# Two blocks of cross attention and experts: where scratch rows are cleared, and how the first context is loaded and normalized

## The chip, the core and the metric

The kernel runs on one core of a Trainium2 chip. The number that counts is the device time of one execution in microseconds (us); lower is better. The core has a matrix engine (TensorE, "PE" in the profile, its weight loads "PEld"), a vector engine (VectorE, "DVE"), a scalar engine (ScalarE, "ACT") and GpSimd ("POOL"). SyncE ("SP") computes nothing here: its instruction queue issues most of the DMA transfers. ACT and POOL issue some as well, from their own queues. All transfers run on the same 16 DMA engines.

## The reference, cut to what matters

```python
x = x + xattn0(ctx, layernorm(x))        # 8 heads of 128; keys from ctx and from x
x = x + experts0(layernorm(x))           # 8 experts, the best 2 of each token, capacity 1024
x = x + xattn1(ctx, layernorm(x))        # 8 heads of 32
x = x + experts1(layernorm(x))           # 8 experts, the best 2 of each token, no capacity
# inside xattn0, for each of 4 batches:
xn, ln = norm(ctx) * gm + bm, norm(latents) * gl + bl
q = ln @ Wq + bq
k, v = split(concat([xn, ln]) @ Wkv + bkv)
out = softmax(q k^T * 128**-0.5) v @ Wo + bo
```

There are 4 batches of 512 rows of x (width 256) and 4 contexts of 1601 rows. Everything is float32. In the first expert layer a slot that no token fills counts as a row of zeros, and in the second each expert's rows have a variable number. So the kernel keeps three scratch arrays in DRAM, which are cleared before tokens are scattered into them.

## The kernel before, in words

The kernel has four stages, one after the other, all in one program.

- **Opening** (lines 541 to 816). Loads of weights, context 0 and x; layer norm of x twice (once for the block, once inside the attention; the result is called lat) and of the 13 tiles of 128 context rows; transposes of both into `kvin`; queries and keys of head 0.
- **First attention** (loop from line 825). A step is one tile of 128 queries of one head of one batch: 4 x 8 x 4 = 128 steps. A step computes `scores` on PE (L735), a row maximum on DVE (L743), the exponential on ACT (L749), then `exchange`: 16 transfers that swap blocks of 32 rows between partitions (L756; 12 issued by SP, 4 by ACT). One step later `turn` transposes the swapped blocks on DVE (L764). `weigh` multiplies a pair of turned tiles with the values (L772, PE). The scores have one PSUM buffer, so scores of a step wait for the exponential of the step before. PE's other work is put between: queries and keys of the next head (L670, L685), values of a pair of heads (L718) and the output projection (L783). The list `later[n]` holds what is added to step n.
- **First experts** (loop at line 1023). For each expert: load `sx`, its 512 slots, from `slot_x` (L1026), transpose, hidden layer (L970), results of the expert before (L983), and two weight loads of 1 MB for the next expert (L909, L910). Results go to `slot_y`.
- **Second attention and second experts** follow. The second experts take rows from `rows_a` and `rows_b`, which are scattered during the second attention.

Three scratch arrays are cleared at the end of the opening. `clear_rows` (L370 to L380) sends 4 transfers of 530 KB for `rows_a` and 37 for `rows_b` from SP, out of a zero tile of 4 x 265 numbers per partition. `clear_slots` (L179) sends 8 transfers of 512 KB for `slot_x` from POOL. The arrays are 19.8, 2.2 and 4.2 MB (`rows_b`, `rows_a`, `slot_x`).

The code does not fix every engine's order. A list scheduler arranges each engine's instructions ahead of the run, by dependencies and by durations that it assumes. Two helpers bind it: `in_order(*engines)` keeps what is traced inside it in program order on those engines, and `keep_in_program_order` puts one instruction behind the one traced before it on its engine. Neither adds a wait for completion. An engine's queue then runs strictly in that order.

The opening of before is free for the scheduler. It uses `ln_moments`, `ln_scale` and `ln_apply` (L111 to L149): statistics of all 13 context tiles, then one scale for all of them, then the normalization, all on DVE except one square root on ACT. The bias of the output is also worked out there: eight times a copy of a bias column over 128 columns (`values_bias`, L801) and a matmul pair with `wo` (L802), summed in one PSUM tile, added to `bo`, and `bo` added to x of batch 0 on POOL (L601).

`keys` (L681 to L697) takes four blocks of 512 contiguous columns of `kvin` and one of 128, and ACT writes each back permuted, since the key order in `kT` is by the position k of a column's 32-group within its block of 128.

Of the kernel before, what the change touches and what calls it, by code (L numbers as in the profile page):

```python
# [8 lines left out]
F32 = mybir.dt.float32  # L9
I32 = mybir.dt.int32  # L10
AF = mybir.ActivationFunctionType
ALU = mybir.AluOpType
# [50 lines left out]
def rows_of(i, n, tail):  # L63
    return tail if i == n - 1 else P
# [3 lines left out]
def xattn_ffn_twice(ctx: ExitStack, tc: tile.TileContext, a: dict, out: bass.AP):  # L68
# [107 lines left out]
    rows_a = dram.tile([E * G, PAY], F32, name="rows_a")  # L176
    rows_b = dram.tile([ROWS + G, PAY], F32, name="rows_b")

    def clear_slots(zeros):  # L179
        for i in range(SLOTS // (4 * P)):  # L180
            nc.gpsimd.dma_start(
                slot_x[i * 4 * P : (i + 1) * 4 * P, :].rearrange("(p r) d -> p r d", p=P), zeros
            )


    iota_i = const.tile([P, NT, E], I32, name="iota_i")
    nc.gpsimd.iota(iota_i, pattern=[[0, NT], [1, E]], base=0, channel_multiplier=0)
    iota = const.tile([P, NT, E], F32, name="iota")
    nc.vector.tensor_copy(iota, iota_i)
# [146 lines left out]
                )  # L336


    lane_i = const.tile([P, 1], I32, name="lane_i")
    nc.gpsimd.iota(lane_i, pattern=[[0, 1]], base=0, channel_multiplier=1)  # L340
    lane = const.tile([P, 1], F32, name="lane")
    nc.vector.tensor_copy(lane, lane_i)
    number_i = const.tile([P, NG], I32, name="number_i")
    nc.gpsimd.iota(number_i, pattern=[[1, NG]], base=0, channel_multiplier=0)
    number = const.tile([P, NG], F32, name="number")
    nc.vector.tensor_copy(number, number_i)
    full = const.tile([P, T // G], F32, name="full")
    nc.vector.tensor_scalar(full, number[:, : T // G], float(G), None, ALU.mult)
    notafter = const.tile([P, E, E], F32, name="notafter")
# [19 lines left out]

    def clear_rows(empty):  # L370

        nc.gpsimd.memset(empty, 0.0)
        nc.gpsimd.memset(empty[:, :, D : D + 1], NOWHERE)
        for rows in (rows_a, rows_b):
            n = rows.shape[0]
            for i in range(0, n, 4 * P):
                some = rows[i : min(i + 4 * P, n), :]
                nc.sync.dma_start(
                    some.rearrange("(p r) d -> p r d", p=P), empty[:, : some.shape[0] // P, :]
                )  # L380

    def route2(b, two, psum, tag, first=0, n=NT):

# [148 lines left out]
    with ExitStack() as st:  # L532
# [9 lines left out]
        gbl = w.tile([P, 2, DC], F32, name="gbl")  # L542
        bqk = w.tile([P, 3, H0], F32, name="bqk")
        bo = w.tile([P, D], F32, name="bo")
        for dst, names in (
            (gbm, ("gamma_media", "beta_media")),
            (gbl, ("gamma_lat", "beta_lat")),
            (bqk, ("bq", "bk", "bv")),
        ):
            for k, name in enumerate(names):  # L550
                nc.sync.dma_start(dst[:, k, :], a[name])
        nc.sync.dma_start(bo, a["bo"].partition_broadcast(P))

        kvin = one.tile([P, DC, NB, 4, 32], F32, name="kvin")
        nc.vector.memset(kvin[:, :, NB - 2 :, 3, :], 0.0)
# [12 lines left out]
            nc.sync.dma_start(t[:TAIL, NM - 1, :], a["ctx"][b, full:, :])  # L568
            return t

        ctx_b = load_ctx(0)

        wq = w.tile([P, DC, INNER], F32, name="wq")
        wkv = w.tile([P, DC, 2 * INNER], F32, name="wkv")
        wo = w.tile([P, H0, D], F32, name="wo")
        nc.sync.dma_start(wq, a["wq"].rearrange("(c p) f -> p c f", p=P))
        nc.sync.dma_start(wkv, a["wkv"].rearrange("(c p) f -> p c f", p=P))
        nc.sync.dma_start(wo, a["wo"].rearrange("(h p) d -> p h d", p=P))
        for b in range(1, B):
            load_x(b)  # L580
        nc.sync.dma_start(wr, a["w_router"].rearrange("(c p) e -> p c e", p=P))
        nc.sync.dma_start(bias, a["bias"].partition_broadcast(P))

        def keys_input(b, ctx_b):

# [11 lines left out]

            def latents_again():
                layernorm(two, state["lat"], state["lat"], NT)
                for i in range(NT):  # L600
                    nc.gpsimd.tensor_tensor(x[b][:, i, :], x[b][:, i, :], bo, ALU.add)  # L601

            def apply(n0):
                for i in range(n0, min(n0 + 4, NM)):
# [38 lines left out]
            def ctx_group(n0):  # L643
                group(ctx_b, n0, min(4, NM - n0), S + n0 * P, gbm, TAIL, NM)


            early = [
                lambda: moments(range(4)),
# [12 lines left out]
        def queries_keys(h):  # L661

            qT = two.tile([P, S], F32, tag="qT", name="qT")
            kT = two.tile([P, LP], F32, tag="kT", name="kT")
            hs = slice(h * DH0, (h + 1) * DH0)

            def queries():
                ps = ps_t.tile([P, 512], F32, tag="t", name="ps_q")
                for c in range(DC):
                    nc.tensor.matmul(  # L670
                        ps,
                        lhsT=wq[:, c, hs],
                        rhs=kvin[:, c, : S // 32, 0, :],
                        start=c == 0,
                        stop=c == DC - 1,
                    )
                nc.vector.tensor_scalar(
                    qT, ps, bqk[:, 0, h : h + 1], DH0**-0.5, ALU.add, ALU.mult
                )

            def keys(j0):  # L681
                n = min(512, LP - j0)
                ps = ps_t.tile([P, 512], F32, tag="t", name="ps_k")
                for c in range(DC):
                    nc.tensor.matmul(  # L685
                        ps[:, :n],
                        lhsT=wkv[:, c, hs],
                        rhs=flat_kvin[c][:, j0 : j0 + n],
                        start=c == 0,
                        stop=c == DC - 1,  # L690
                    )
                nc.scalar.activation(  # L692
                    kT.rearrange("p (k b i) -> p b k i", k=4, i=32)[:, j0 // P : (j0 + n) // P],
                    ps[:, :n].rearrange("p (b k i) -> p b k i", k=4, i=32),
                    AF.Identity,
                    bias=bqk[:, 1, h : h + 1],
                )  # L697

            return qT, kT, [queries] + [lambda j0=j0: keys(j0) for j0 in range(0, LP, 512)]


        parts = (range(0, NB // 2 + 1), range(NB // 2 + 1, NB))
# [77 lines left out]
        def project(oT, inv, h, b, half):  # L780
# [9 lines left out]
            for k in range(2):  # L790
# [3 lines left out]
                    xs, ps[:, k, :], inv[:, t : t + 1], xs, ALU.mult, ALU.add  # L794
                )


        values_bias = w.tile([P, P], F32, name="values_bias")
        ps = ps_t.tile([P, D], F32, tag="t", name="ps_bo")
        for h in range(H0):  # L800
            nc.vector.tensor_copy(values_bias, bqk[:, 2, h : h + 1].to_broadcast([P, P]))  # L801
            nc.tensor.matmul(  # L802
                ps, lhsT=values_bias, rhs=wo[:, h, :], start=h == 0, stop=h == H0 - 1
            )
        nc.vector.tensor_tensor(bo, bo, ps, ALU.add)

        early, late = keys_input(0, ctx_b)
        for s in early + late:
            s()
        *qk, fill = queries_keys(0)  # L810
        for s in fill:
            s()
        empty = one.tile([P, 4, PAY], F32, tag="lat", name="empty")
        clear_rows(empty)
        clear_slots(empty[:, :, :D])
        load_second()

# [1 line left out]
        later = [[] for _ in range(n_steps + 4)]  # L821
        tiles = {}
        v_of = [None, None]
        early = late = ()
        for n in range(n_steps + 4):
            b, h, t = n // (H0 * NT), n // NT % H0, n % NT
# [166 lines left out]
    with ExitStack() as st:  # L993
# [20 lines left out]
        def results(e, hT, w2):  # L1014
# [4 lines left out]
                slot_y[e * CAP : (e + 1) * CAP, :].rearrange("(t p) d -> p t d", p=P), y  # L1019
            )  # L1020

        last = None
        for e in range(E):
            w1, w2 = w_next
# [9 lines left out]
            last = (e, hT, w2)  # L1034
            if e + 1 < E:
                w_next = expert_weights(wexp, "w1", "w2", e + 1)
        results(*last)

        got0, steps = collect(0)
        for f in steps:  # L1040
# [721 lines left out]
```

## Time and profile before

| | us |
|---|---|
| median of 3 runs | 2993.43 (2989.96 to 2995.0) |
| the profiled execution's own time | 2993.88 |
| its span | 2992.2 |
| PE busy in the span | 2778.0 (93%) |
| DVE busy | 1456.4 (49%) |
| ACT busy | 933.3 (31%) |
| first scores of the first attention start | 53.06 |
| first attention ends, first experts begin (about) | 1635 |
| first hidden layer of the first experts starts | 1706.9 |
| last result of the first experts lands (about) | 1939 |

The profiled execution is within 0.5 us of the median. Its own time is 1.7 us above its span, for what lies around it. PE busy says how long PE had a matmul in flight, not that it ran at its peak. A row of a group gives line, engine, tile written and tiles read, number of instructions, busy time, and the idle time of the engine just before them with what ended it. A queue's row (SPq, ACTq) gives the time in which that queue was issuing transfers, not the time of the transfer itself.

### The profile page before, as it was taken

The numbers are of one execution on the slowest core, as the hardware profiler recorded it, in microseconds if no ns is written. First come the engines' busy times: TensorE is split into PE (matmuls) and PEld (weight loads), VectorE is DVE, ScalarE is ACT, GpSimd is POOL, SyncE is SP. The second block draws the span as 40 slices with busy tenths as digits, with TensorE's granted clock in tenths as the row PEclk, the third lists the DMA queues.
The fourth block names the chain that finished last, engine by engine and source line by source line (L and its number), as shares of the span: only waits on it lengthen the run. The fifth ranks groups of instructions, "written<-read, shape, count | busy, mean of one in ns | idle before, by whom it ended". The sixth has DMA issues, their size and how long they took to land.

```text
span 2992.2 us, 35534 instructions
## 1 busy us (share of the span) xinstructions
PE 2778.0 (93%) x13426; PEld 1839.3 (61%) x13426; DVE 1456.4 (49%) x2324; ACT 933.3 (31%) x1312; POOL 400.0 (13%) x308
## 2 busy tenths in 40 slices
PE   5699999999999999999997999879989898898998
PEld 2466676667766667666665566634444444466887
DVE  4256447544475444554454200178777768741110
ACT  2133234323343233333331221124434344341221
POOL 1000000100001000000000100022314223333442
PEclk9899999999999999999998899979999999898999
DMA  8743334433344333333334333110101110055552
GB/s 297 236 124 95 98 92 103 117 92 89 95 113 109 90 94 91 99 93 97 95 94 120 117 106 115 47 46 17 28 24 41 29 37 23 11 181 169 185 173 72
DMA packets 165103, 295.95 MB, mean 99 GB/s; under 512 B 43287, under 2 KB 81752, under 8 KB 161848
## 3 DMA queue, kind: packets, MB, share of 16 engines
q1 hardware_dynamic: 124024, 204.45, 24.4%
q0 software_dynamic: 16320, 53.42, 5.9%
q10 hardware_dynamic: 24576, 35.68, 4.6%
q8 instruction: 109, 1.79, 0.3%
q14 instruction: 74, 0.61, 0.1%
HBM read 97.86 MB, written 49.76 MB: 49 GB/s over the span
## 4 chain that ended last, share of the span: by engine, by line
PE 82%; DVE 7%; issue 3%; DMA 3%; ACT 3%; SPq 2%; POOL 1%; POOLq 0%; DVEq 0%; ACTq 0%
PE ps_o L772 15%; PE ps_s L735 15%; PE ps_v L718 7%; PE ps_k L685 7%; PE ps_w L1188 6%; PE ps_y L1470 4%; PE ps_h L1451 4%; PE ps_h L970 4%; PE ps_y L983 4%; DVE tops L1149 2%; PE ps_o L1219 2%; DVE sum L1210 2%; PE ps_p L783 2%; PE ps_v L945 2%; PE ps_q L670 2%
## 5 line engine op out<-in xcount | busy, mean ns | idle before, releaser
L743 DVE TENSOR_REDUCE top<-ps_s 128x1 f32<-128x2113 f32 x128 | 301.8, 2358 | 574.8 <-PE ps_s L735 574.8
L772 PE MATMUL ps_o<-pT,v 128*128 128x256 f32 x2176 | 521.5, 382 | 7.7 <-DVE pT L764 7.7
L735 PE MATMUL ps_s<-kT,qT 128*128 128x512 f32 (+1 forms) x1280 | 488.9, 527 | 26.3 <-ACT attn L749 26.0
L772 PEld LDWEIGHTS ps_o<-pT,v 128*128 128x128 f32 x2176 | 411.4, 191 | 124.8 <-issue 70.3
L735 PEld LDWEIGHTS ps_s<-kT,qT 128*128 128x128 f32 x1280 | 241.8, 191 | 275.7 <-issue 239.9
L749 ACT ACTIVATE attn<-ps_s,top 128x2113 f32<-128x2113 f32 x128 | 259.0, 2024 | 486.5 <-DVE top L743 448.8
L764 DVE STREAM_TRANSPOSE pT<-swapped 128x2176 f32<-128x2176 f32 x128 | 312.4, 2441 | 70.8 <-DMA swapped<-attn 60.3
L1149 DVE TENSOR_REDUCE tops<-ps_s 128x2 f32<-128x1024 f32 (+1 forms) x224 | 237.4, 1104 | 135.2 <-PE ps_s L1138 135.0
L685 PE MATMUL ps_k<-kvin,wkv 128*128 128x512 f32 (+1 forms) x640 | 262.0, 534 | 5.0 <-ACT kT L692 5.0
L1188 PE MATMUL ps_w<-asked,keyed 64*128 64x256 f32 (+1 forms) x1664 | 244.2, 415 | 20.5 <-DVE tops L1149 9.5
L718 PE MATMUL ps_v<-wkv,kvin 128*128 128x256 f32 x1088 | 253.5, 381 | 0.0
L1201 ACT ACTIVATE pT<-ps_w 128x1024 f32<-128x1024 f32 (+1 forms) x176 | 179.5, 1024 | 192.5 <-PE ps_w L1188 190.4
L1188 PEld LDWEIGHTS ps_w<-asked,keyed 64*128 64x128 f32 (+1 forms) x1664 | 147.0, 189 | 143.2 <-ACT pT L1201 60.7
L718 PEld LDWEIGHTS ps_v<-wkv,kvin 128*128 128x128 f32 x1088 | 204.9, 190 | 32.7 <-issue 3.3
L1210 DVE TENSOR_TENSOR sum<-sum,pT 128x1024 f32<-128x1024 f32 (+1 forms) x128 | 181.0, 1414 | 10.7 <-ACT pT L1201 3.9
L692 ACT ACTIVATE kT<-ps_k,bqk 128x512 f32<-128x512 f32 (+1 forms) x160 | 97.3, 621 | 268.7 <-DMA swapped<-attn 129.8
L1210 POOL TENSOR_TENSOR sum<-sum,pT 128x1024 f32<-128x1024 f32 x48 | 124.1, 2585 | 345.7 <-ACT pT L1201 345.5
L685 PEld LDWEIGHTS ps_k<-kvin,wkv 128*128 128x128 f32 x640 | 116.5, 192 | 80.9 <-issue 67.1
L1451 PE MATMUL ps_h<-xT,w_e 128*128 128x256 f32 x640 | 143.9, 383 | 10.2 <-issue 10.2
L1138 PE MATMUL ps_s<-kT,qT 32*128 32x512 f32 (+1 forms) x1024 | 140.5, 577 | 12.5 <-ACT kT L936 6.8
L725 ACT COPY v<-ps_v 128x512 f32<-128x512 f32 x144 | 80.0, 561 | 224.9 <-PE ps_v L718 156.2
L1470 PE MATMUL ps_y<-w_e,hT 128*128 128x256 f32 x640 | 144.4, 385 | 0.0
(261 smaller groups left out, 2615.1 us busy)
## 6 DMA issues: line engine op xcount, KB each, us to landing
swapped<-attn SPq DMA_DIRECT2D x1536, 68.0 KB
swapped<-attn ACTq DMA_DIRECT2D x512, 68.0 KB
rows_b<-empty SPq DMA_DIRECT2D x36, 530.0 KB
w<-in_w_dram SPq DMA_DIRECT2D x16, 1024.0 KB
w_e<-in_wall_dram SPq DMA_DIRECT2D x7, 2052.0 KB
cT<-in_ctxT_dram SPq DMA_DIRECT2D x4, 1601.0 KB
keyed<-kT SPq DMA_DIRECT2D x32, 200.1 KB
ctx_b<-in_ctx_dram SPq DMA_DIRECT2D x4, 1536.0 KB
```

The costliest lines, as they stand in the source:

```text
L685: nc.tensor.matmul(ps[:, :n], lhsT=wkv[:, c, hs], rhs=flat_kvin[c][:, j0 : j0 + n], start=c == 0, stop=c == DC - 1,)
L718: nc.tensor.matmul(ps[:, k, :], lhsT=flat_kvin[c][:, j * P : (j + 1) * P], rhs=wkv[:, c, cols], start=c == 0, stop=c == DC - 1,)
L735: nc.tensor.matmul(flat[:, j0 : j0 + n], lhsT=qT[:, t * P : (t + 1) * P], rhs=kT[:, j0 : j0 + n], start=True, stop=True,)
L743: nc.vector.tensor_reduce(top, flat[:, :L], AX.X, ALU.max, negate=True)
L749: nc.scalar.activation(attn[:, :L], flat[:, :L], AF.Exp, bias=top, accum_out=total)
L764: nc.vector.transpose(pT[:, :, k * P : (k + 1) * P].rearrange("p c (a i) -> p a c i", a=4), swapped.rearrange("p a (c i) -> p a c i", i=32),)
L772: nc.tensor.matmul(ps, lhsT=v[:, j - parts[part][0], (h % 2) * DH0 : (h % 2 + 1) * DH0], rhs=pT[:, j, :], start=j == 0, stop=j == NB - 1,)
L1149: nc.vector.tensor_reduce(tops[u][:, t : t + at // n, 2 * pair : 2 * pair + 2, j0 // 512], of, AX.X, ALU.max,)
L1188: nc.tensor.matmul(ps[:r, s, pair * QH : (pair + 1) * QH], lhsT=keyed[o][64 * s : 64 * s + 64, pair, j * P : j * P + r], rhs=asked[u % 3][ ...
L1210: (nc.gpsimd if k else nc.vector).tensor_tensor(to, to, pT[:r], ALU.add)
L1451: nc.tensor.matmul(ps[:, f, :], lhsT=w(at, P), rhs=xT[:, c, :], start=c == 0, stop=c == DC - 1,)
L1470: nc.tensor.matmul(ps, lhsT=hT[:, f, r * P : (r + 1) * P], rhs=w(WB1 + f * D, D), start=f == 0, stop=f == FC - 1,)
```

## The change

The clearing of the three scratch arrays is put elsewhere, and the opening is written anew.

- `clear_slots` is now called eight times, in steps 4, 6, ... 18 of the first attention, and issued by SP instead of POOL, each call pinned behind SP's instruction traced before it. The zeros are one tile of 256 numbers per partition, repeated four times by the transfer.
- `clear_rows` is now a generator. The loop over the first experts takes six of its 41 transfers after the weight loads of each next expert. They stay on SP, pinned in the same way; the zeros are one row of 265 numbers per partition, repeated four times.
- The loads of the opening are traced in a given order on SP: x, the first four context tiles, the small vectors, the columns of head 0 of `wq` and `wkv`, the other context tiles, then the remaining weights, x of the other batches and the router.
- Layer norm of context 0 is done in groups of four tiles (`first`): statistics and scale on DVE, the normalization itself on ACT (scale and bias of one ACTIVATE).
- PE, DVE, ACT and POOL run the opening in program order. Keys are cut by k, so that the first block of keys needs the latents alone.
- The bias of the output, with its eight copies and matmul pairs and the POOL addition for batch 0, moves to step 13 of the first attention.
- Three small integer tiles get a pool of their own that is closed early.

```diff
-    def clear_slots(zeros):
-        for i in range(SLOTS // (4 * P)):
-            nc.gpsimd.dma_start(
-                slot_x[i * 4 * P : (i + 1) * 4 * P, :].rearrange("(p r) d -> p r d", p=P), zeros
+    def clear_slots(zeros, i):
+        tc.keep_in_program_order(
+            nc.sync.dma_start(
+                slot_x[i * 4 * P : (i + 1) * 4 * P, :].rearrange("(p r) d -> p r d", p=P),
+                zeros.unsqueeze(1).to_broadcast([P, 4, D]),
             )
...
     def clear_rows(empty):
-        nc.gpsimd.memset(empty, 0.0)
-        nc.gpsimd.memset(empty[:, :, D : D + 1], NOWHERE)
...
-                nc.sync.dma_start(
-                    some.rearrange("(p r) d -> p r d", p=P), empty[:, : some.shape[0] // P, :]
-                )
+                tc.keep_in_program_order(
+                    nc.sync.dma_start(
+                        some.rearrange("(p r) d -> p r d", p=P),
+                        empty.unsqueeze(1).to_broadcast([P, some.shape[0] // P, PAY]),
+                    )
+                )
+                yield
...
+        loading.enter_context(in_order(nc.sync))
+        for n0 in range(0, NM - 1, 4):
+            nc.sync.dma_start(ctx_b[:, n0 : n0 + 4, :], of_ctx[:, n0 : n0 + 4, :])
+            if n0 == 0:
+                load_vectors(gbl, "gamma_lat", "beta_lat")
+                load_vectors(bqk, "bq", "bk", "bv")
+                nc.sync.dma_start(wq[:, :, :DH0], of_wq[:, :, :DH0])
+                nc.sync.dma_start(wkv[:, :, :DH0], of_wkv[:, :, :DH0])
+                load_vectors(gbm, "gamma_media", "beta_media")
+        nc.sync.dma_start(ctx_b[:TAIL, NM - 1, :], a["ctx"][0, (NM - 1) * P :, :])
+        nc.sync.dma_start(wkv[:, :, INNER:], of_wkv[:, :, INNER:])
+        nc.sync.dma_start(wq[:, :, DH0:], of_wq[:, :, DH0:])
+        nc.sync.dma_start(wkv[:, :, DH0:INNER], of_wkv[:, :, DH0:INNER])
...
+            def first(n0):
+                n = min(4, NM - n0)
+                mv = two.tile([P, 4, 2], F32, tag="mv4", name="mv_g")
...
+                for i in range(n):
...
+                    nc.vector.bn_stats(st[:r], ctx_b[:r, n0 + i, :])
+                    nc.vector.bn_aggr(mv[:r, i, :], st[:r])
+                mv, rs = ln_scale(two, mv, 4)
+                away = two.tile([P, 4], F32, tag="nt4", name="away")
+                nc.vector.scalar_tensor_tensor(away, mv[:, :, 0], -1.0, rs, ALU.mult, ALU.mult)
+                for i in range(n):
...
+                    nc.scalar.activation(
+                        of, of, AF.Identity, scale=rs[:r, i : i + 1], bias=away[:r, i : i + 1]
+                    )
...
-            def keys(j0):
-                n = min(512, LP - j0)
+            def keys(k):
+                n = 512 if k < 4 else P
...
-                        rhs=flat_kvin[c][:, j0 : j0 + n],
+                        rhs=kvin[:, c, : NB - 1, k, :] if k < 4 else kvin[:, c, NB - 1, :, :],
...
-        early, late = keys_input(0, ctx_b)
-        for s in early + late:
+        opening.enter_context(in_order(*computing))
+        latent, context = keys_input(0, ctx_b)
+        *qk, fill = queries_keys(0)
+        stats, turns = context[::2], context[1::2]
+        for s in (
+            latent[:2] + stats[:1] + latent[2:] + fill[:2] + stats[1:2] + turns[:1] + stats[2:3]
+            + turns[1:2] + fill[2:3] + stats[3:] + turns[2:3] + fill[3:4] + turns[3:] + fill[4:]
+        ):
             s()
...
-        clear_rows(empty)
-        clear_slots(empty[:, :, :D])
...
+        for i in range(SLOTS // (4 * P)):
+            later[4 + 2 * i].append(lambda i=i: clear_slots(empty, i))
+        later[13].append(output_bias)
...
+        clear = clear_rows(empty)
         last = None
         for e in range(E):
...
             if e + 1 < E:
                 w_next = expert_weights(wexp, "w1", "w2", e + 1)
+                for _ in range(6):
+                    next(clear, None)
         results(*last)
```

In the order of the opening, `latent` is the layer norm, the second layer norm and the transposes of the latents, `stats` the four groups `first`, `turns` the transposes of the four groups, and `fill` the queries and the five blocks of keys of head 0.

## The prediction, made before the changed kernel was run

> **What bounds the kernel now.** I read the chain of waits first, cut to the first stretch, because the page's share of "DMA 3%" is a mean over four unlike stages.
>
> ```profile
> by line: DMA rows_b<-empty 25.7%; SPq L378 25.6%; PE ps_s L735 14.8%; PE ps_o L772 8.1%; DMA swapped<-attn 6.9%; ACT attn L749 4.7%; PE ps_k L685 4.3%; DVE top L743 3.9%; SPq L756 3.4%; issue 2.5%; PE ps_p L783 0.8%; ACTq L749 0.1%
> ...
> 44.59 18.01 DMA rows_b<-empty
> ...
> 62.62 12.86 DMA rows_b<-empty
> ...
> 100.49 1.25 SPq L378
> ...
> 101.84 6.37 DMA swapped<-attn
> ```
>
> This is the chain from 40 to 160 us (start, length, what). Half of it is the clearing of `rows_b`: SP is issuing those transfers until 101.8, and only then the first exchange. The timeline shows who pays:
>
> ```profile
> 53.06 3.87 PE L735 MATMUL ps_s<-kT,qT 128*128 128x512 f32 x10 [0.33 <-ACT kT L692]
> ...
> 65.48 6.27 ACTq L756 DMA_DIRECT2D swapped<-attn  x4
> ...
> 71.81 1.26 ACT L692 ACTIVATE kT<-ps_k,bqk 128x512 f32<-128x512 f32 x2 [9.76 <-DMA swapped<-attn]
> ...
> 80.57 14.97 PE L718 MATMUL ps_v<-wkv,kvin 128*128 128x256 f32 x68
> ...
> 101.84 33.56 SPq L756 DMA_DIRECT2D swapped<-attn  x42
> 115.11 2.44 DVE L764 STREAM_TRANSPOSE pT<-swapped 128x2176 f32<-128x2176 f32 x1 [31.99 <-DMA swapped<-attn]
> ...
> 117.33 5.83 PE L735 MATMUL ps_s<-kT,qT 128*128 128x512 f32 x10 [18.35 <-ACT attn L749]
> ```
>
> ACT is held in its own queue while DMA is full, keys wait for ACT; `turn` waits 32 us; PE stands still 18.35 us. Last, the windows (length, then busy time of PE, PEld, DVE, ACT, POOL, then PE clock, DMA share, GB/s):
>
> ```profile
> 53.06:141.80 88.74, 59.66 (x185) 36.40 (x185) 20.78 (x15) 20.65 (x28) 0.00 (x0) 0.85 0.81 280
> ...
> 200.00:400.00 200.00, 200.00 (x743) 137.12 (x742) 111.23 (x153) 67.71 (x91) 2.97 (x4) 1.00 0.41 103
> ...
> 1740.00:1760.00 20.00, 19.99 (x77) 13.40 (x76) 1.96 (x4) 3.29 (x6) 0.00 (x0) 1.00 0.37 114
> ```
>
> After 141.8 PE is never idle in the attention, so time lost before it comes off the end in full, and work added to PE is added in full. The first experts (last line) are PE-bound with DMA 37% busy.
>
> **What the Trainium skill says.** "DMA: Bandwidth & Descriptors", section Queues, rings and completion order: on each DMA engine the descriptors of one queue are consumed in ring order. The trace agrees: exchanges came behind the clears on SP. Its section Issuing engines are not separate DMA queues says all issuers share 16 engines; agreed: ACT's four transfers took 6.27 us to issue at 65.48 and 2.71 at 141.77. "ScalarE: Activation LUTs", section Table sets, says identity is in every table set, so the new ACTIVATE between square roots loads no table; the trace has Identity (L630) between a root and the load at 53.28, with no load of its own. "TensorE: Matmul & The Clock Gate", What's actually happening, says PE is at half clock after about 3.4 us idle; here the ten score matmuls took 5.83 us after the 18 us stall against 3.87 before.
>
> **Step 1, stall in the first steps.** From 53.06 to 141.80 PE computed, counted at the pace of the undisturbed stretch (from 153.90 a score group starts the next after 3.60; four key matmuls 1.72, eight value matmuls 1.73, six `ps_o` 1.29): five score groups 18.0, queries and keys (28 large matmuls of 0.43, four small of 0.11) 12.4, values (68 of 0.216) 14.7, `ps_o` (34 of 0.216) 7.3. Sum 52.4. Lost: 88.7 - 52.4 = 36.3 us.
> What is late next? The pipeline's own filling. A score cycle is 3.87 + 2.36 (maximum) + 2.1 (exponential) = 8.4 us. Counting from the first scores: exponential 0 ends at 8.4, keys of head 1 fill PE to about 9; scores 1 to 12.8; more keys to 16.8; exponential 1 ends at 17.4 (0.6 lost); scores 2 to 21; values fill 14.7, to 36. An exchange takes 9.7 us in the undisturbed part (exponential ends 141.75, `turn` at 151.47), so tile 1 is turned at about 30, before PE wants it. At least 0.6 us is lost. If the scheduler keeps the order of before (values and next queries ahead of scores 3, then scores 4 close behind), the gaps of 4.60 and 1.09 before 127.76 and 141.80 stay. I take 4, bounds 0.6 and 9. Gain: 32.3 (27.3 to 35.7).
>
> **Step 2, the opening.** In before DVE waits for context until 13.69, while x was in by about 4.3 (the windows show 376 GB/s in 3 to 4 us, then a lull of 21). After, DVE starts on x at 4.3. Rows: statistics 0.41 and aggregate 0.17 with the next overlapped, about 0.52 a tile; the chain of scale, 0.2 + root 0.24 + five small operations of 0.17, 1.27; application 0.34 a tile. One layer norm of x: 2.1 + 1.27 + 1.37 = 4.75; two end at 13.8. First context group on DVE 2.1 + 1.27 + 0.16 = 3.5, to 17.4; ACT applies four tiles at 0.36 (a COPY of 128x256 at 141.64) to 18.9, then the latents' half to 19.7 (0.78, L630). Queries 1.72 us on a warm PE; it had 8 transposes only, so half clock, 3.0, to 22.7; DVE writes them (0.75) by 23.5. Next group: DVE to 27.1, ACT to 28.5, evacuations (1.0 on each) to 29.5. Third: DVE to 31.6, ACT 33.1, evacuation 34.1; keys 1 to 35.9 and out by 36.7. The last tile's root stands behind that on ACT: applied by 38.3, evacuation of group 2 by 39.3; keys 2 to 41.1, last evacuation 42.6; keys 3 and 4 to 44.9, written by 45.5. First scores at 45.5 against 53.06: gain 7.5. Bounds: 42 (warm PE, overlap everywhere) and 50 (0.1 us more at each of some 40 hand-overs). The loads don't decide: 7.9 MB at some 380 GB/s are in by 25, values' weights needed beyond 65.
>
> **Step 3, the bias in step 13.** In before its matmuls lay in PE's idle opening. Now 16 matmuls of 0.216 stand in the PE-bound loop: 3.45 us. The single copy buffer makes each pair wait for a copy (0.23) that waits for the pair before: the pairs from 34.58 came 1.08 apart with 0.70 busy, so up to 8 x 0.65 above the steady pace if nothing is put between. It also holds one of two PSUM buffers that keys need. Cost 5, bounds 3.45 and 9. DVE (111 of 200 us busy) and POOL (idle) hide the copies and four additions of 0.73.
>
> **Step 4, eight slot clears on SP.** POOL issued them in 0.97 us each. On SP, 0.4 to 1.25 to issue, and 512 KB at about 345 GB/s (the x loads, 1 KB rows, at 22 us) is 1.5 us on DMA, every second step. Behind them stands the next step's exchange; behind that `turn`, and DVE's queue. A step lasts 12.4 us ((1635 - 53)/128) and SP issues 12 x 0.59 = 7.1 of it, so there is room. Cost 0; 8 x 2.7 = 22 if the cover were gone each time.
>
> **Step 5, 41 row clears among the experts.** An expert takes 28.7 us on PE. After a second weight load SP is free:
>
> ```profile
> 1749.53 0.37 SPq L910 DMA_DIRECT2D w<-in_w_dram  x1
> 1749.99 0.54 SPq L1018 DMA_DIRECT2D slot_y<-y  x1
> 1750.63 0.45 SPq L1026 DMA_DIRECT2D sx<-slot_x  x1
> 1764.83 0.37 SPq L909 DMA_DIRECT2D w<-in_w_dram  x1
> ```
>
> Six clears (3.2 MB in rows of 1060 bytes) take 6 x 1.25 = 7.5 us to issue at the pace of before, 9.3 us of DMA at 345 GB/s, beside 3 MB of weights and slots (7.9 at 380): 17 of 28.7. The next w load comes 14 us later; a first-layer weight issued at 1764.83 is used at 1808, `sx` from 1750.63 at 1807, so a delay of 9 us reaches nobody. Six clears may be issued already after 1640, behind the first loads in the ring; they end by about 1661, before the scatter of 1677. Cost 0. The repeated source is not in this trace: at below 3.2 MB in 20.8 us (153 GB/s) the stage would become DMA-bound.
>
> **Sum.** -32.3 - 7.5 + 5 = -34.8; on the profiled time 2993.88, 2959.1. That time is 0.45 above the median, which changes nothing. Predicted 2959.
>
> **Rivals.**
> 1. Forecast, 0.68: 2959; its own range from the bounds, 2951 (-35.7 - 11 + 3.45 = -43) to 2973 (-27.3 - 3 + 9 = -21).
> 2. The opening gains nothing, 0.14: strict order makes DVE, ACT and PE wait for one another where the free order overlapped them; each group's 9 us round would have to grow by 2. For it: DVE was busy without a gap from 13.69 to 30. Against: DVE sheds 13 tile applications (4.4 us) and starts 9 us sooner. 2993.9 - 32.3 + 5 = 2967.
> 3. The clears move the wait, 0.10: slot clears delay exchanges of steps 4 to 18 by all of 22 us. For: SP carries 57% already; against: the slack above. 2959 + 22 = 2981. The change not doing what it says belongs here: pins hold the clears back, but nothing holds other transfers in front.
> 4. Slower, 0.05: row clears out of a repeated source run far below 345 GB/s. At a quarter, six take 37 us, with 7.9 of loads 45 in a 28.7 us expert; 7 x 16.6 = 116: 3075. It turns the result once each of seven experts loses 5 us, below about 124 GB/s. For it: four times the descriptors of 4240 bytes. Against: slots in 1 KB pieces were cleared in before with DMA at 347 GB/s or more from 38 on.
> 5. Gain greater, 0.03: PE never waits and the bias is hidden: -36 - 11 + 3 = -44: 2950.
>
> **Numbers.** Range 2949 to 2975: cases 1, 2 and 5, some 0.85. A change under 0.2% (6 us) can't be told from none. Faster 0.93 (1, 2, 3, 5, less a little), same 0.02, slower 0.05.
>
> **What would show it.** First scores near 45.5; no PE wait above 5 us in the first five steps and SP issuing exchanges from the first exponential on; `ps_bo` matmuls in step 13 with 3 to 9 us more there; experts still 28.7 us apart, and DMA near 60% between them. I am wrong if experts spread, if PE waits in steps 4 to 18, or if the first scores stay at 53.

## The result, and the profile after

The changed kernel takes 2974.12 us (median of 4 runs, 2973.21 to 2975.36) where the kernel before took 2994.22 beside it (2989.96 to 2997.24): a ratio of 0.9925, with a 95% interval of 0.9913 to 0.9938. That is 20.1 us less; 34.8 were forecast. The profiled execution has its own time of 2973.3 and a span of 2971.6.

The chain of waits of the changed kernel can't be followed back beyond its last transfers (it begins at 2949.81), so the timeline has to answer. This is the timeline of the changed kernel from 40 to 142 us, over all engines (start, length, engine, line, operation, tile written and tiles read, count, and in brackets the idle time before it with what ended it):

```profile
54.90 54.50 SPq L811 DMA_DIRECT2D swapped<-attn  x60
54.90 3.65 ACTq L811 DMA_DIRECT2D swapped<-attn  x4
...
64.97 2.71 ACTq L811 DMA_DIRECT2D swapped<-attn  x4
...
65.00 5.57 PE L790 MATMUL ps_s<-kT,qT 128*128 128x512 f32 x10 [2.04 <-ACT attn L804]
...
68.56 2.45 DVE L819 STREAM_TRANSPOSE pT<-swapped 128x2176 f32<-128x2176 f32 x1 [0.25 <-DMA swapped<-attn]
...
76.44 1.13 PE L790 MATMUL ps_s<-kT,qT 128*128 128x512 f32 x2 [0.65 <-ACT attn L804]
```

SP issues exchanges from the first exponential on, ACT needs 3.65 and 2.71 us for its four where 6.27 stood before, and DVE waits 0.25 us for the first swapped block in place of 31.99. PE's 18.35 us are gone. What is late next is the exponential: PE waits 2.04 us for it, and after the wait it runs at half clock (5.57 us for ten score matmuls that take 3.87 else).

The windows of the changed kernel (start and end, length, then busy time of PE, PEld, DVE, ACT and POOL, PE clock, DMA share, GB/s):

```profile
66.14:69.56 3.42, 3.42 (x5) 1.36 (x5) 3.09 (x10) 1.80 (x3) 0.00 (x0) 0.50 0.78 198
...
50.36:141.80 91.44, 88.27 (x305) 56.43 (x305) 55.78 (x91) 35.65 (x45) 0.00 (x0) 0.98 0.42 107
...
200.00:400.00 200.00, 200.00 (x762) 137.47 (x761) 101.20 (x108) 64.53 (x88) 5.75 (x8) 1.00 0.41 104
...
1749.00:1777.00 28.00, 27.99 (x104) 18.71 (x103) 2.39 (x5) 5.36 (x9) 0.00 (x0) 1.00 0.96 226
```

The first line is the half clock after the wait. From the first row maximum to 141.80 PE is busy 97% of the time, where it was 67% from the first scores to there; the attention is PE-bound as before. The last line holds a surprise: in the first experts DMA is 96% busy at only 226 GB/s, where 60% was forecast. PE doesn't notice.

The two profiles, landmark by landmark (gain in us, profiled executions; the last landmark is the start of the last transfer with which POOL adds results to the output):

| from | to | before | after | gain |
|---|---|---|---|---|
| start | first row maximum | 56.96 | 50.36 | 6.6 |
| first row maximum | last projection of the attention | 1578.19 | 1551.05 | 27.1 |
| last projection | first hidden matmul of the experts | 71.76 | 73.67 | -1.9 |
| first hidden matmul | first `ps_w` of the second attention | 273.95 | 274.28 | -0.3 |
| first `ps_w` | last `ps_w` | 660.96 | 668.11 | -7.2 |
| last `ps_w` | last output addition on POOL | 339.91 | 340.43 | -0.5 |
| last output addition | end of the span | 10.42 | 13.68 | -3.3 |

At the end of the first attention 33.7 us have been gained, 1.1 less than the whole forecast. Then 13.1 are lost, in stages that the forecast took as unchanged. The sum is 20.6.

### The profile page after: what moved, and what is told of

Same layout as the page of the kernel before. It is cut to its first block, busy times and chain, and to the rows that moved or that the text cites. A ratio compares the mean times of both kernels' runs of the same rounds, so it can differ in the third digit from the quotient of the medians.

```text
span 2971.6 us, 35547 instructions
## 1 busy us (share of the span) xinstructions
PE 2785.2 (94%) x13426; PEld 1842.2 (62%) x13426; DVE 1457.9 (49%) x2333; ACT 941.9 (32%) x1330; POOL 393.4 (13%) x301
## 5 line engine op out<-in xcount | busy, mean ns | idle before, releaser
L1275 ACT ACTIVATE pT<-ps_w 128x1024 f32<-128x1024 f32 (+1 forms) x176 | 179.5, 1024 | 195.7 <-PE ps_w L1262 193.7
```

Of the source, the lines that this page charges most:

```text
L1275: nc.scalar.activation(pT[:r], ps[:r], AF.Exp)
```

## The experiments

Three questions: is it the moved clears that bring the gain; what do the moved clears and the bias cost where they are now; and what takes 13 us back behind the attention? Times are given with the ratio to the kernel before on the same chip.

**Both kernels again.** No edit.

> The kernel before, unchanged, for a second profile. Up to the end of the first attention the change gained 33.7 us in the profiles, after it 13.1 us were lost: from the last projection of the attention to the end of the span it is 1357.1 us in the profile of before and 1370.2 in that of the changed kernel, with the same order of instructions on DVE. Theory 'clock' (the half-speed spells of PE after idle gaps fall differently in each execution, and so does the tail): that stretch differs from 1357 by some us here, anywhere from 1354 to 1371; the last projection still starts within 1 us of 1635. Theory 'systematic' (the change itself lengthens the later stages): it repeats 1357 within 1.5 us.

> The changed kernel, unchanged, for a second profile and a closer time. Both theories: last projection of the attention at 1601.4 within 1 us, ratio near 0.993. Theory 'clock': the stretch after it differs from 1370.2 by some us, down to 1357. Theory 'systematic': it repeats 1370 within 1.5 us, at least 10 us more than in the second profile of before.

The kernel before gave 2996.55 in its one run. The changed one gave 2972.5 (2967.77 to 2974.01), ratio 0.9915 (0.9902 to 0.9929). The attention ended at 1636.17 and 1602.38, again 33.8 apart. The end of the program took 10.15 and 13.78 us, the second attention 661.08 and 666.92. From the end of the attention to the end of the span it was 1358.7 and 1368.6 us, after 1357.0 and 1370.2 in the first profiles. Both came 1.6 nearer to each other, a little more than the second theory allows; but of the 13.1 us 9.9 are there again, so the loss is in the main not an accident of one profile.

**Only the clears moved**, in the kernel before:

```diff
-        clear_rows(empty)
-        clear_slots(empty[:, :, :D])
+        for i in range(SLOTS // (4 * P)):
+            later[4 + 2 * i].append(lambda i=i: clear_slots(empty, i))
...
+                for _ in range(6):
+                    next(clear, None)
```

> The kernel before with only the clears moved (slots on SP in steps 4 to 18, rows among the experts); loads, layer norm, key cuts and bias as before. By the steps of the prediction the first scores stay at 53 and the last projection of the attention comes 30 to 32 us earlier than in before (near 1604), nearly as early as with the whole change, since the bias stays in the opening. Rival (the gain is mainly the new opening): less than 20 us earlier. If row clears among the experts cost time, first hidden layers come more than 28.9 us apart.

2975.24 us, 0.9927 (0.9912 to 0.9942). The attention ends at 1605.92, 29.2, 30.3 and 32.4 us sooner than in the three profiles of before (1635.15, 1636.17 and, in a third run below, 1638.32).

**Only the opening**, the reverse edit in the changed kernel:

> The changed kernel with the clears put back at the end of the opening, slots on POOL, rows on SP, out of a zero tile of four rows as in before; new loads, layer norm by groups, key cuts and bias in step 13 stay. By the steps of the prediction the stall stays: SP issues row clears until about 90 to 100 us and PE waits more than 12 us for an exponential; the last projection comes 3 to 12 us earlier than in before. Rival (the opening is the gain): 20 us or more earlier.

2996.71 us, 1.0 (0.9992 to 1.0009). The first maximum comes at 51.81, 5 to 7 us earlier than before, and the stall stays, as expected. But the attention ends at 1634.69, only 0.5, 1.5 and 3.6 us earlier than in the three profiles of before, mostly below what was expected. Its timeline (PE's rows, then SP's) tells where the rest is:

```profile
112.46 5.95 PE L786 MATMUL ps_s<-kT,qT 128*128 128x512 f32 x10 [25.28 <-ACT attn L800]
...
137.04 3.87 PE L786 MATMUL ps_s<-kT,qT 128*128 128x512 f32 x10 [1.09 <-ACT attn L800]
```

```profile
44.95 49.79 SPq L382 DMA_DIRECT2D rows_b<-scrap  x37
```

In the kernel before the row of 137.04 is this one:

```profile
141.80 3.87 PE L735 MATMUL ps_s<-kT,qT 128*128 128x512 f32 x10 [1.09 <-ACT attn L749]
```

The wait of 18.35 us of the kernel before is now 25.28: scores that are ready sooner wait longer for the first exchange. But the row clears, begun later, had all been issued 7 us sooner as well (by 94.74 in place of 101.74), and the last wait of the stall ended at 137.04 in place of 141.80 (142.62 and 144.41 in the other profiles of before). Some 5 to 7 us of the opening came through, and the moved bias, 3.45 us or a little more (see below), takes most of them before the attention ends. With the clears moved, opening and bias together gain 3.5 to 4.5 us (1605.92 to 1602.38 and 1601.41), with the old clears 0.5 to 3.6. Whether the two parts add is not settled by this: the three profiles of before alone spread over 3.2 us.

**Slot clears on POOL's queue.** In steps 4 to 18 as in the changed kernel:

```diff
-            nc.sync.dma_start(
+            nc.gpsimd.dma_start(
                 slot_x[i * 4 * P : (i + 1) * 4 * P, :].rearrange("(p r) d -> p r d", p=P),
```

> The changed kernel with one word different: the eight slot clears are issued by POOL (its own DMA queue, as in the kernel before), still in steps 4 to 18. Theory A, that the longer end of the changed kernels (13.7 us from the last output addition to the end of the program, 10.1 to 10.4 in the two forms whose slot clears are on POOL's queue) comes from POOL's queue carrying 15168 packets in place of 16320: the end goes back to 10.1 to 10.5 us, POOL's last drain from 4.84 to 2.60 us, and the kernel is some 3 us faster than the changed one (2970 where that takes 2973.5). Rival B, that the longer end comes from what SP issued or from the place of the row clears: 13.7 us stays and the time is that of the changed kernel within 2 us. In both the attention ends at 1600 to 1604, as the slot clears cost nothing on either queue.

2969.42 us, 0.9904 (0.9887 to 0.9921). The end takes 10.22 us: theory A. These are the lines of part 3 of the page (queue, packets, MB, share of 16 engines), of the changed kernel and of this one:

```profile
q0 software_dynamic: 15168, 49.23, 5.6%
```

```profile
q0 software_dynamic: 16320, 53.42, 6.0%
```

With POOL's queue as full as before, POOL's last drain takes 2.60 us in place of 4.84, and the two increments ahead of it 0.82 and 0.78 in place of 1.36 and 1.33, to the hundredth what the kernel before has. The kernel with only the clears moved, whose slot clears SP issues, has the long end too (13.74 us). So the 3.3 us follow which queue takes the slot clears; why fewer packets on POOL's queue mean a longer end isn't shown.

But the attention ended at 1604.32 in place of 1601.4 to 1602.4, which was not expected. From this kernel's timeline, all engines:

```profile
217.96 2.78 POOL L608 TENSOR_TENSOR x<-x,bo 128x256 f32<-128x256 f32 x4 [197.13 <-DVE bo L861]
...
220.68 2.20 POOL L181 DMA_DIRECT2D slot_x<-scrap  x3
...
228.03 2.20 DVE L147 TENSOR_SCALAR lat<-x,mv,rs 128x256 f32<-128x256 f32 x4 [4.79 <-DMA slot_x<-scrap]
228.06 1.13 PE L838 MATMUL ps_p<-wo,oT 128*128 128x256 f32 x4 [0.79 <-ACT oT L962]
```

POOL runs in order. Three clears stood behind its additions of the output bias, and these waited for `ps_bo` in step 13. The clears read `scrap`, whose buffer is the next batch's `lat`; so DVE stood 4.79 us in front of the layer norm, a row maximum behind it came late, and PE lost 0.79 and then 1.83 us.

**The bias left out.** The sixteen `ps_bo` matmuls, the copies, the addition to `bo` and the four additions to batch 0 are left out.

```diff
-        later[13].append(output_bias)
```

> The changed kernel without the whole of output_bias: the sixteen ps_bo matmuls with their copies, the addition to bo, and the four additions of bo to the first batch's tiles are left out (so the output lacks the output bias in part). Theory A, that the bias in step 13 costs just its matmuls on a PE that is never idle there: the attention ends 3.45 us sooner than in the changed kernel (1598 in place of 1601.4 to 1602.4), and 3.45 us come off the time, give or take the 2 to 3 us by which the second attention varies. Rival B, that the pairs stretch the step by waiting for their copies, or hold a buffer that the keys need: 5 to 9 us. Rival C, that the loop had slack there: 0 to 1 us.

2965.71 us, 0.9902 (0.9885 to 0.992); the attention ends at 1596.97, and from the first maximum to there it takes 4.0 to 4.4 us less than in the two profiles of the changed kernel. In the changed kernel's PE timeline a pair stands like this:

```profile
211.31 0.59 PE L858 MATMUL ps_bo<-wo,scrap 128*128 128x256 f32 x2
211.74 1.02 PE L739 MATMUL ps_k<-kvin,wkv 128*128 128x512 f32 x2
```

Each pair moves the next instruction by 0.43 us, eight times 3.45, and its copy is made under a key or score pair; no PE idle time is shown. That is theory A, at the low bound of the forecast or a little above.

**The statistics drawn ahead in the opening.**

```diff
-            latent[:2] + stats[:1] + latent[2:] + fill[:2] + stats[1:2] + turns[:1] + stats[2:3]
-            + turns[1:2] + fill[2:3] + stats[3:] + turns[2:3] + fill[3:4] + turns[3:] + fill[4:]
+            latent[:2] + stats[:1] + latent[2:] + stats[1:2] + fill[:2] + turns[:1] + stats[2:3]
+            + turns[1:2] + stats[3:] + fill[2:3] + turns[2:3] + fill[3:4] + turns[3:] + fill[4:]
```

> The changed kernel with two places of the opening's written order exchanged: the statistics of the second and of the last context group come ahead of queries and of the first keys' input. In the trace of the changed kernel DVE stood 4.21 us behind the query's evacuation at 23.6 and 3.99 us behind the last tile's root at 38.6. Theory A, that these two waits hold the opening: first maximum at 45 to 47 in place of 50.4 to 51.7, the attention ends 4 to 6 us sooner (1596 to 1598), and the time is 4 to 6 us less, 2968 to 2970. Rival B, that the pipeline's filling takes back what the opening gains (as it did with the old clears, where the opening's 7 us became 1): first maximum earlier, but the attention ends within 2 us of 1601.4, and the time stays at 2972 to 2975.

2966.13 us, 0.9895 (0.9879 to 0.9912). The first maximum comes at 48.22 (2.1 to 3.5 us sooner, less than expected) and the attention ends at 1598.56, sooner by the same 2.9 to 3.8. So what this order gains in the opening reaches the end of the attention; rival B falls. The time fell by more than that, but the interval overlaps that of the changed kernel's second measurement (from 0.9902).

**Every row clear sent twice.**

```diff
-        for rows in (rows_a, rows_b):
+        for rows in (rows_a, rows_a, rows_b, rows_b):
...
-                for _ in range(6):
+                for _ in range(12):
```

> The changed kernel with every row clear sent twice, twelve behind each expert's weights in place of six, so that the cost of the row clears doubles if they have one. Theory A, that they cost nothing because the expert stage is bound by PE with DMA to spare (7.9 us of weights and slots and 2 x 9.3 us of clears are 26.5 of the 28.7 us of an expert): from the first hidden matmul of the first experts to the first of the second attention's ps_w stays at 273.9 to 274.4 us, DMA near 90% there, and the time is that of the changed kernel plus 0 to 4 us. Rival B, that the clears already delay weights or slot reads a little: that stretch grows by 5 us or more, and what it grows by is what the six clears are near to costing. If the repeated source were slow, 45 us or more would be added.

3011.29 us, 1.0051 (1.0035 to 1.0068): slower than the kernel before. The experts' stretch took 309.26 us in place of 274.28, so theory A's sum of 26.5 us an expert was far off. Once the queue has filled, PE waits in its timeline:

```profile
1844.19 1.94 PE L161 MATMUL tp<-ident,sx 128*128 128x128 f32 x8 [5.90 <-DMA sx<-slot_x]
...
1921.86 16.12 PE L1050 MATMUL ps_y<-w,hT 128*128 128x256 f32 x64 [4.89 <-DMA w<-in_w_dram]
```

Is it the rate of the clears, or SP's queue? Two variants, both with a source of four distinct rows a partition, sent twice. The first has only the change of source and writes 4240 contiguous bytes; the second has the change of target as well and writes four rows that lie 128 rows apart:

```diff
-                        empty.unsqueeze(1).to_broadcast([P, some.shape[0] // P, PAY]),
+                        empty[:, : some.shape[0] // P, :],
...
-                        some.rearrange("(p r) d -> p r d", p=P),
+                        some.rearrange("(r p) d -> p r d", p=P),
```

> Every row clear sent twice as in the run before it, but out of a source of four whole rows a partition (as in the kernel before), so that source and target are both contiguous over 4240 bytes. With one row repeated the trace had DMA 94% busy at 223 GB/s in the experts of the changed kernel and 214 GB/s where clears ran alone; with four whole rows the kernel before moved 398 GB/s. Theory A, that the pieces of 1060 bytes halve the rate and that this is what stretched the experts when the clears were doubled: twelve clears are 6.5 MB, 16.3 us at 398 GB/s, with 3.1 MB of weights and slots about 25 of 28.7 us; from the first hidden matmul to the second attention 273.9 to 276 us in place of 309, and the time 2972 to 2977. Rival B, that SP's queue and not the rate was too full (twelve issues and what stands behind them): still 300 us or more, 3005 to 3012.

> As the run before (twelve clears an expert, a source of four rows a partition, each row distinct), but the target written with the four rows of a partition 128 rows apart, so that every piece is 1060 bytes although the source is not repeated. Theory A1, that the length of the pieces sets the rate: as with the repeated source, about 210 GB/s and DMA over 100% busy, the experts' stretch 300 to 310 us, 3005 to 3012. Rival A2, that reading one row again and again sets it: 274 to 276 us and 2972 to 2977.

Whole rows: 2973.18 us, 0.9909 (0.9893 to 0.9926), the experts' stretch 273.97. Twice the clears cost nothing. Short pieces: 2977.71 us, 0.9927 (0.991 to 0.9944), the stretch 281.25. Windows in the experts with doubled clears, from the run with the repeated row, the one with whole rows and the one with short pieces:

```profile
1770.00:1805.00 35.00, 34.98 (x135) 24.56 (x134) 3.24 (x7) 5.36 (x9) 0.00 (x0) 1.00 1.10 242
```

```profile
1749.00:1777.00 28.00, 27.99 (x104) 18.73 (x103) 2.39 (x5) 5.36 (x9) 0.00 (x0) 1.00 0.93 343
```

```profile
1749.00:1777.00 28.00, 27.99 (x102) 18.39 (x102) 2.38 (x5) 5.36 (x9) 0.00 (x0) 1.00 1.09 295
```

So it is not the number of issues on SP's queue; it is the rate. Doubled clears of 6.51 MB with 3.15 MB of weights and slots need 9.66 / 28.7 = 337 GB/s on average. Whole rows reach 343 with DMA to spare; short pieces reach 295 at full load and lose 7 us; one row repeated reaches 242 and loses 35. With short pieces PE has no wait for DMA inside the experts: most of the 7 us comes at their end, where the last results leave SP behind the clears (PE's wait there is 26.72 us, 21.04 in the changed kernel).

Neither rival of the second variant holds alone. Between 1624 and 1632, where clears ran nearly alone, the three moved 228, 407 and 237 GB/s: there the short pieces explain the whole loss. Beside weights and slots the repeated row is slower again (242 against 295). Why it is slower only there is not shown, and the two runs also differ in the order in which rows are written.

**The kernel before a third time**, for the second attention.

> The kernel before, unchanged, for one more profile. From the first to the last ps_w of the second attention it took 660.96 and 661.08 us in two profiles, while nine profiles of changed kernels spread over 661.8 to 668.1. Theory A, that the stage's length is chance (where PE's granted clock falls to half there): any value from 661 to 668. Rival B, that the kernel before is always at the low end and the change in itself costs some 5 us there: 660.5 to 661.5.

Its one run took 3001.29 us, span 2999.57. From the first to the last `ps_w` it needed 666.74 us: theory A, for this stage taken alone. The PE timelines of before and of before the third time at the same place of the stage:

```profile
1986.66 5.65 PE L1138 MATMUL ps_s<-kT,qT 32*128 32x512 f32 x20 [0.47 <-DVE tops L1149]
1992.32 2.27 PE L1188 MATMUL ps_w<-asked,keyed 64*128 64x256 f32 x16
```

```profile
1992.78 6.60 PE L1138 MATMUL ps_s<-kT,qT 32*128 32x512 f32 x20 [0.47 <-DVE tops L1149]
1999.31 3.79 PE L1188 MATMUL ps_w<-asked,keyed 64*128 64x256 f32 x16
```

The same matmuls after the same 0.47 us of idle time run at full clock in one execution of a kernel and at half clock in another execution of the same kernel, and the changed kernel has the slow pattern to the hundredth (6.60 and 3.79 us). The windows over the whole stage, before, before the third time, and changed:

```profile
1980.87:2641.83 660.96, 590.21 (x4982) 310.35 (x4982) 494.36 (x757) 279.52 (x332) 205.22 (x117) 0.95 0.10 27
```

```profile
1986.88:2653.62 666.74, 595.76 (x4981) 313.21 (x4982) 494.40 (x757) 279.52 (x332) 203.12 (x117) 0.93 0.10 27
```

```profile
1949.36:2617.47 668.11, 596.80 (x4981) 314.14 (x4982) 494.49 (x757) 279.54 (x332) 204.59 (x117) 0.93 0.10 27
```

The work is the same on every engine; PE's busy time and clock differ. The kernel without moved clears ("only the opening") took 666.79 as well; the ten profiles with moved clears lie between 661.84 and 668.12, eight of them above 663.5. The Trainium skill, "TensorE: Matmul & The Clock Gate", section What's actually happening, says that the activity window that sets the clock is free-running, so that where a stretch of work falls in it is chance; the same matmuls at two clocks in two executions of one kernel agree.

But this chance does not explain the loss behind the attention. In the third profile of before the stage was 5.8 us longer, and the next, to the last output addition, 4.1 us shorter (335.78 in place of 339.91). The two stages have to be taken together:

| clears | profiles | first `ps_w` to last output addition |
|---|---|---|
| in the opening: before (three times), "only the opening" | 4 | 999.4 to 1002.6, mean 1001.3 |
| moved: all other kernels | 10 | 1002.1 to 1010.7, mean 1006.5 |

The changed kernel has 1008.5 and 1006.3. So with the clears moved some 5 us more are spent in the second attention and the second experts, although the order of instructions there is the same on every engine, before and changed. What causes that stays open: no run tests it.

**Joined.** The drawn-ahead statistics; the slot clears on POOL in steps 4 to 11, so ahead of the bias; the row clears out of four whole rows.

```diff
-            later[4 + 2 * i].append(lambda i=i: clear_slots(empty, i))
+            later[4 + i].append(lambda i=i: clear_slots(empty, i))
```

> What the runs point to, in one kernel: the opening's order with the statistics of the second and the last context group drawn ahead; the slot clears on POOL's queue in steps 4 to 11, so that all are issued ahead of the additions of the output bias (behind those they kept a buffer of the second batch from DVE, and PE waited 0.79 and 1.83 us at 228 and 235); the row clears, once each, out of four whole rows. Expected from the parts: attention end at 1598 to 1600 as with the new order alone, the end 10.2 us in place of 13.5, DMA in the experts about 0.65 busy in place of 0.95 with no gain in time; together 2963 (2960 to 2967), against 2966 with the order alone and 2973 for the changed kernel. If the slot clears still hold something up on POOL, the attention ends 2 to 3 us later and the time is that of the order alone.

2961.98 us (2956.76 to 2965.87), 0.9868 (0.9851 to 0.9884), as expected, beside 3000.8 of before; the run with twice the clears in whole rows, which was as fast as the changed kernel, took 2973.18 on the same chip. The attention ends at 1599.39, the end takes 10.43 us. This is faster than both kernels. SP's queue in the experts, first in the changed kernel, then here (in both the clears and what stands behind them):

```profile
1718.80 9.15 SPq L383 DMA_DIRECT2D rows_b<-empty  x6
1728.05 2.47 SPq L1097 DMA_DIRECT2D sx<-slot_x  x1
```

```profile
1716.94 4.00 SPq L383 DMA_DIRECT2D rows_b<-empty  x6
1722.33 0.37 SPq L1097 DMA_DIRECT2D sx<-slot_x  x1
```

And the window of an expert here:

```profile
1749.00:1777.00 28.00, 27.98 (x104) 18.74 (x103) 2.39 (x5) 5.23 (x9) 0.00 (x0) 1.00 0.62 223
```

Nearly the same bytes a second with DMA 62% busy in place of 96%.

## Why the prediction was right, and what it got wrong

The direction, the mechanism and the place of the gain were right; of the gain of 34.8 us some 10 to 15 did not arrive, and the measured time, 2974.1, lies at the upper edge of the range. That it lies inside, by 0.9 us, is luck in part: the range allowed for a worse stall, opening and bias, and what was lost was lost elsewhere. Step by step:

1. **The stall** (forecast 32.3). At the end of the attention 33.7 us are gained; without the opening's 6.6 and with the bias's 3.45 paid, 30.6 are left for the stall, so 5.7 of the 36.3 us stay lost where 4 were taken. The rows show 4.9 of it: waits of 0.48, 2.04 and 0.65, and 1.70 for ten matmuls at half clock. The count by paces was sound; the half clock after a short wait was missing. The forecast quoted some 3.4 us of idle time for it; here a wait of 2.04 us was followed by half clock from 66.14 to 69.56, and the measurement decides. "Only the clears" confirms the step by itself with 29 to 32 us.
2. **The opening** (7.5). 6.6 by the first maximum: the forecast's first scores at 45.5 with 3.9 us for them would have put it at 49.4, and it came at 50.36. Steps 2 and 3 together make 2.5 (7.5 less 5), and "only the opening" ended its attention 0.5 to 3.6 sooner. The two order stalls on DVE, 4.21 and 3.99 us, were not in the forecast's chain; a changed order took back 2 to 4 of the 8.
3. **The bias** (5). 3.45 by the rows, 4.0 to 4.4 by leaving it out. No pair waits for its copy: a key or score pair stands between.
4. **Slot clears on SP** (0). In the attention right: they are issued in 0.59 us each and land in 3.3 to 3.9, and PE is never idle in steps 4 to 18. But taking them off POOL's queue lengthened the end of the program by 3.3 us. The forecast counted every instruction that moved and not the queue that it left.
5. **Row clears among the experts** (0). Right in its result, by a margin that it had wrong. It reckoned 9.3 us of DMA for six clears, at the 345 GB/s of other transfers, and 60% in all; the trace has 96%. That is the mechanism of the slower rival, a repeated source in short pieces, at about 230 GB/s: above the 124 at which the rival put its turn, yet near the edge, since DMA at 96% leaves about 1 us an expert. The doubled clears went over it. Against that rival the forecast had said that slots went "in 1 KB pieces" at 347 GB/s or more in the kernel before. That was misread: of the 2238 packets of its trace between 30 and 60 us 231 are under 512 bytes and just these 231 under 2 KB, so the slots crossed in larger packets and were no evidence about short pieces. That the clears cost nothing even so was luck.
6. **The sum** is the step that failed: "-34.8; on the profiled time 2993.88" carries the gain to the end as if all behind the attention would take what it took in that one profile of before. Of the 13.1 us lost there, 3.3 are the end of the program, which the change causes (step 4). The 1.9 ahead of the experts is within what that stretch varies (71.76 to 74.74 in three profiles of before). The second attention and the second experts together lost 7.7 in this pair of profiles and 5.2 on average over all (1006.5 against 1001.3), with the cause open. The medians miss it too: 33.7 less 3.3 would be 30.4 us, and 20.1 and 24.2 were measured. So the profiled time being 0.45 from the median, which the forecast said "changes nothing", was no safeguard: it told that this one execution was typical, not that the later stages would stay as they were.

The rivals: the opening that gains nothing, and clears that move the wait, would have given times near the measured one (2967 and 2981), but the landmarks exclude both. That is worth seeing: a total alone would have pointed to the wrong cause.

## What to carry to other kernels

A stall at a full DMA is worth only what the next late thing leaves. Work made earlier in front of it can seem to be worth nothing: look at where the stall ends, and at what else the change added behind it, before saying that the gain was swallowed, and test the parts singly and together. When a transfer is hidden behind other work, look at its rate in its new form, not only at its bytes; contiguous pieces on both sides kept the margin that short repeated ones used up. And when a gain is carried through later stages that the change does not touch, do not take them as fixed: measure them in several profiles of both kernels, and over stretches long enough that one stage's loss is not the next one's gain.

## What the runs showed of the hardware

- Clears of 530 KB a transfer into DRAM, nearly alone on the DMA engines, moved 407 GB/s in pieces of 4240 bytes, and 228 to 237 in pieces of 1060. The Trainium skill, "DMA: Bandwidth & Descriptors", section Specifications, puts the least size for line rate at 512 B; pieces of 1060 bytes did not reach the rate of the longer ones here, and the measurement decides. The slot clears, 1024 bytes a piece out of a repeated row, moved about 350 GB/s around 111 us, so the length alone isn't the rule. 1060 is no multiple of 256, and 1024 is; that this is the cause wasn't tried.
- With eight transfers fewer on POOL's queue the end of the program took 3.3 us more (POOL's drain 4.84 us against 2.60), in every run of either kind.
- The second attention varied by 5.8 us between profiles of the same kernel with the same work on every engine; 5.5 of it is PE's busy time (590.21 and 595.76 us), at a granted clock of 0.95 and 0.93.
- A PE wait of 2.04 us was followed by 3.42 us at half clock.
